# A gated block behind a selective scan: what follows the first norm is re-timed, and the last two units' work is rearranged

## The chip, the cores and the metric

The kernel runs on one core of one Trainium2 chip. The metric is the device time of one execution in microseconds. Five engines work side by side: TensorE (PE; PEld is its weight load), VectorE (DVE), ScalarE (ACT), GpSimd (POOL), and SyncE (SP), which issues nearly all DMA transfers. Each engine takes its instructions strictly in the order in which the program lists them. An instruction that waits holds up everything behind it on its engine.

## The reference

The input x is 4 sequences of 1024 rows of 256 numbers, all float32. In short:

```python
def _mamba(u, ...):                       # u = rmsnorm(layernorm(x))
    z, x, Bc, Cc, dt_raw = split(u @ in_proj_w.T)
    dt = softplus(dt_raw @ dt_proj_w.T + dt_proj_b)
    h = exp(dt_t * A) * h + (dt_t * x_t) * B_t      # step by step over the 1024 rows
    y_t = sum over 32 states of h * C_t
    return ((y + x * D_param) * silu(z)) @ out_proj_w.T

h = u0 + _mamba(rmsnorm(u0)); xn = rmsnorm(h)       # u0 = layernorm(x)
a = h + (silu(xn @ gate_w.T) * (xn @ up_w.T)) @ down_w.T
x = x + a
v = layernorm(x)
hidden = fwht(silu(v @ W1.T) * (v @ W3.T))          # 1024 wide
x = x + hidden @ W2.T
```

The Walsh-Hadamard transform is folded into W2 once, at the start.

## The kernel before

**Units.** The 4096 rows are cut into 8 units of T = 512 rows (`us`), two to a sequence. The second unit of a sequence (units 1, 3, 5, 7, "odd") carries the scan's state over from the first ("even").

**The scan.** 256 channels by 32 states by 512 rows are too much for one tile, so each unit's scan is 16 quarters (`q`, 128 in all). A quarter holds four tiles of 128 lanes by 512 rows (`da`, 128x2048). A quarter takes two *ticks*. In each tick DVE multiplies u by B for two of the four tiles (`bx`, line 765) and runs two scans (line 774). So a unit is 32 ticks and the whole scan is ticks 0 to 255. The text counts ticks within the unit that is being scanned, t0 to t31. Around a quarter:

- SP loads `da` (dt spread over lanes, 1 MB) into one of four buffers, three quarters ahead (`dma_da`), and `ub` in halves.
- ACT turns `da` into exp(dt*A), two tiles a tick, one quarter ahead (line 741).
- POOL multiplies the scanned quarter by C in one instruction (`times_c`, line 784), in the even tick that follows the scan. In even units it first copies the last column to `carry` (line 783).
- PE sums over the states in the odd tick after that (`sum_states`, line 795, "the sum" below). The sum frees the `da` buffer, so the next load of `da` waits for it.
- Every eighth quarter a new B has to be in PSUM (`pb`, one buffer). `copy_b` (line 754) copies it in t15 and t31: before, DVE did it in t15 and ACT in t31.

**Everything else.** It is written into the same ticks with `at(tick, lane, function)`. In a tick the lanes are issued in a fixed order: PE, ACT, the tick's `bx`, ACTb, two exps, a scan, DVE, a scan, POOL0, `times_c`, POOL, the sum, PEend, ACTend, SP, the scan's loads, SPend. So the order on every engine is set by hand. The work is of two kinds:

- `pre(u, H)`: what a unit needs before its scan, which starts at tick H. LayerNorm and first rmsnorm of x in one (`row_stats`, `small`, `un`), transposes (`ut`), the projections `pe_x`, `pe_dt`, `pe_c`, and the transfers through DRAM that spread rows over lanes (`dma_xb`, `dma_xr`, `dma_dt`, `dma_u`, `dma_c`). All of it runs during the scan one and two units earlier.
- `post(u, E, other)`: what follows a unit's scan, which ended at tick E. `wo` (with `add_rows`), `row_stats` and `small2` (rmsnorm), `hn`, transposes (`ht`), two `gated` calls for gate and up (product `m`), `wd` by `add_rows`, the second LayerNorm (`small3`, `hn`, `xt`), three `gated` calls for W1 and W3 (product `g`), W2 by `add_rows` in four blocks of 128 rows, and `store`. This runs during the scan of the next unit, and for the last unit after all scans (the *tail*). `gated` also computes z of the unit `other`.

A `gated` call puts its projections (two matmul instructions each) two to a tick on PE, the silus on ACT a tick later, the copies `up` (line 270) two ticks later and the products on POOL (line 274) two and three ticks later. Silu, Exp and Softplus need an activation table load when ACT goes from one to another.

`add_rows` can bring its result into `hr` in two ways: DVE adds out of PSUM (line 316), or ACT copies it out (`evict`, line 321) and POOL adds (line 325).

**What the buffers tie.** PSUM: four `dense` banks in rotation, two for `bx`, one for `pb`, one for the sums. `big` (m, then g) has one buffer, `tok` (un, hn) has one, `T` (ut, ht, yt, xt) has three.

In before, offsets in `post` are written from E and those in `pre` from H: gated m at E+10 and E+13, wd at E+18, gated g at E+26, E+29, E+32, W2 at E+36, store at E+43; `un` at H-32, its transposes at H-30, `pe_x` at H-24, `dma_xr` at H-19 and H-17, `pe_dt` and the first `pe_c` at H-16. With E = H = a multiple of 32 these are t10, t13, t18, t26, t29, then t0, t4 to t7, t11; and t0, t2, t8, t13, t15, t16.

Of the kernel before, what the change touches and what calls it, by code (L numbers as in the profile page):

```python
# [27 lines left out]
def tile_block(ctx: ExitStack, tc: tile.TileContext, a, out):  # L28
# [130 lines left out]
        nc.scalar.mul(w2h[:, k : k + 2, :], pw, 1.0 / 32.0)  # L159


    def row_stats(u, src, ts, centred=True):

        if 0 in ts:
            u["mv"] = sm.tile([P, 2, TT], F32, tag="mv", name="mv")
        for t in ts:
            junk = p1.tile([P, DM], F32, tag="junk", name="junk")
            nm, ms = u["mv"][:, 0, t : t + 1], u["mv"][:, 1, t : t + 1]
            if centred:
                nc.scalar.activation(  # L170
                    junk, src[:, t, :], AF.Identity, scale=-1.0 / (16 * DM), accum_out=nm
                )
            nc.scalar.activation(  # L173
                junk,
                src[:, t, :],
                AF.Square,
                bias=nm if centred else 0.0,
                scale=1.0 / 16,
                accum_out=ms,
            )  # L180
# [64 lines left out]
    def gated(tick, u, dst, wa, wb, chunks, src, z=None):  # L245


        g = [{} for _ in chunks]
        pe_z, act_z = z[0]["z"] if z else (None, None)

        def pe(i, name, w):
            c, n = chunks[i]
            if n < P:

                both = project(W[w], c * P, 2 * n, u[src])
                g[i]["pg"], g[i]["pu"] = both, both[n:]
            else:
                g[i][name] = project(W[w], c * P, n, u[src])

        def silus():  # L260
            for i, (_, n) in enumerate(chunks):
                g[i]["si"] = p3.tile([P, T], F32, tag="si", name="si")
                nc.scalar.activation(g[i]["si"][:n], g[i]["pg"][:n], AF.Silu)  # L263
            if z:
                act_z(z[1])

        def up(i):
            n = chunks[i][1]
            g[i]["up"] = p3.tile([P, T], F32, tag="up", name="up")
            nc.scalar.copy(g[i]["up"][:n], g[i]["pu"][:n])  # L270

        def product(i):
            c, n = chunks[i]
            nc.gpsimd.tensor_tensor(u[dst][:n, c, :], g[i]["si"][:n], g[i]["up"][:n], ALU.mult)  # L274

        three = len(chunks) == 3
        steps = [(i, *s) for s in (("pg", wa), ("pu", wb)) for i in range(len(chunks))]
        steps = [s for s in steps if chunks[s[0]][1] == P or s[1] == "pg"]
        late = z and len(steps) == 6
        steps = [(pe, *s) for s in steps]  # L280
        if z:
            steps.insert(3, (pe_z, z[1]))
        for k, step in enumerate(steps):
            at(tick + k // 2, "PE", *step)
        at(tick + 1, "ACTend" if three else "ACT", silus)
        at(tick + 2, "ACT", up, 0)
        for i in range(1, len(chunks)):
            if i == 2 and late:
                at(tick + 3, "ACT", up, i)
            else:  # L290
                at(tick + 2, "ACTend", up, i)
        at(tick + 2, "POOL", product, 0)
        for i in range(1, len(chunks)):
            at(tick + 3, "POOL", product, i)

    def add_rows(tick, u, lhs, rhs, per_tick, lane="PE", on_pool=False):

        po = {}

# [25 lines left out]
            nc.gpsimd.tensor_tensor(hr, hr, po[i][0], ALU.add)  # L325

        for t in range(TT):
            at(tick + t // per_tick, lane, pe, t)
            if t % 2:
                after = tick + t // per_tick + 1  # L330
                if on_pool:
                    at(after, "ACTend", evict, t // 2)
                    at(after + 1, "POOL", add_pool, t // 2)
                else:
                    at(after, "DVE", add, t // 2)


    def pre(u, H):
# [218 lines left out]
            return  # L557
        if H == 32:

            at(0, "ACTend", lambda: row_stats(u, u["x"], (0, 1)))  # L560
            at(1, "ACTend", lambda: row_stats(u, u["x"], (2, 3)))
            at(3, "POOL", small)
            at(5, "POOL", small_end)
            at(4, "ACT", un, (0, 1))
# [2 lines left out]
            at(6, "ACTend", transposed, u, "ut")  # L567
        else:
            at(H - 54, "SP", load_x, u)
            at(H - 45, "ACTend", lambda: row_stats(u, u["x"], (0, 1)))  # L570
            at(H - 43, "ACTend", lambda: row_stats(u, u["x"], (2, 3)))
            at(H - 39, "POOL", small)
            at(H - 37, "POOL", small_end)
            at(H - 32, "ACT", un, (0, 1))
            at(H - 31, "ACT", un, (2, 3))
            at(H - 30, "PE", lambda: transposes(u, s["un"]))
            at(H - 30, "ACTend", transposed, u, "ut")
        at(H - 24, "PE", pe_x)
        at(H - 23, "ACT", act_x)
        at(H - 22, "SP", dma_xb)  # L580
        at(H - 19, "SPend", dma_xr, 0)
        at(H - 17, "SPend", dma_xr, 1)
        at(H - 16, "PE", pe_dt)
        at(H - 16, "PE", pe_c, 0)
        if H == 32:
            for h in range(2):
                at(H - 11, "PE", pe_z, h)
# [16 lines left out]
    def post(u, E, other):  # L604


        s = {}

        def hr(ts):
            if 0 in ts:  # L610
# [20 lines left out]
            scaled_rows(s["tok"], u["hr"], s[scale], s[bias] if bias else None, range(TT))  # L631

        def big(name):
            u[name] = p1.tile([P, 8, T], F32, tag="big", name=name)

        def store():
            b, c = u["b"], u["c"]
            nc.sync.dma_start(
                out=out[b, c * T : (c + 1) * T, :].rearrange("(t p) d -> p t d", p=P), in_=u["hr"]
            )  # L640

        at(E + 3, "ACT", hr, (0, 1))
        at(E + 4, "ACT", hr, (2, 3))
        add_rows(
            E + 3,
            u,
            lambda: [u["yt"][:, k, :] for k in range(2)],
            lambda: [W["wo"][:, k, :] for k in range(2)],
            4,
            "PEend",  # L650
            on_pool=u is not us[-1],
        )
        at(E + 5, "ACTend", lambda: row_stats(u, u["hr"], (0, 1), False))
        at(E + 6, "ACTend", lambda: row_stats(u, u["hr"], (2, 3), False))
        at(E + 7, "POOL", small2)
        at(E + 8, "ACT", hn, "r3", None)
        at(E + 9, "PE", lambda: transposes(u, s["tok"]))
        at(E + 9, "ACTend", transposed, u, "ht")
        at(E + 9, "POOL", lambda: nc.gpsimd.tensor_tensor(u["hr"], u["hr"], u["x"], ALU.add))
        at(E + 10, "PE", big, "m")  # L660
        sizes = [min(P, DFF - c * P) for c in range(6)]
        chunks = list(enumerate(sizes))
        for i in range(2):
            gated(E + 10 + 3 * i, u, "m", "wg", "wu", chunks[3 * i : 3 * i + 3], "ht",
                  (other, i) if other else None)
        add_rows(
            E + 18,
            u,
            lambda: [u["m"][:n, c, :] for c, n in enumerate(sizes)],
            lambda: [W["wd"][:n, c, :] for c, n in enumerate(sizes)],  # L670
            1,
        )
        at(E + 20, "ACTend", lambda: row_stats(u, u["hr"], (0, 1)))
        at(E + 22, "ACTend", lambda: row_stats(u, u["hr"], (2, 3)))
        at(E + 23, "POOL", small3)
        at(E + 24, "ACT", hn, "r4", "nm")
        at(E + 25, "PE", lambda: transposes(u, s["tok"]))
        at(E + 25, "ACTend", transposed, u, "xt")
        at(E + 26, "PE", big, "g")
        chunks8 = [(c, P) for c in range(8)]  # L680
        for i in range(3):
            gated(E + 26 + 3 * i, u, "g", "w1", "w3", chunks8[3 * i : 3 * i + 3], "xt")
        add_rows(
            E + 36,
            u,
            lambda: [u["g"][:, c, :] for c in range(8)],
            lambda: [w2h[:, c, :] for c in range(8)],
            1,
            on_pool=u is not us[-1],
        )  # L690
        at(E + 43, "SPend", store)


    an = nega.rearrange("p (h j b a) -> p h j b a", h=2, j=4, b=4)
# [53 lines left out]
    def carry_of(s):  # L748
        return s["u"]["carry"][:, s["h"], s["j"], :, s["g"]]

    def copy_b(q):
        u, h = qs[q]["u"], qs[q]["h"]
        u["pb"] = ps_b.tile([P, T], F32, tag="b", name="pb")
        (nc.vector.tensor_copy if h else nc.scalar.copy)(u["pb"], u["br", h])  # L754

    def times_b(q, b0):
        s = qs[q]
# [15 lines left out]
        start = 0.0 if u["c"] == 0 else carry_of(s)[:, b : b + 1]  # L773
        nc.vector.tensor_tensor_scan(da, da, s["bx"][:, b % 2, :], start, ALU.mult, ALU.add)  # L774

    def times_c(q):
        s = qs[q]
        u = s["u"]
        if u["c"] == 0:
# [1 line left out]
                kept = p2.tile([P, 2, 4, 4, 2], F32, tag="carry", name="carry")  # L781
                u["carry"] = us[us.index(u) + 1]["carry"] = kept
            nc.gpsimd.tensor_copy(carry_of(s), s["da"][:, :, T - 1])
        nc.gpsimd.tensor_tensor(  # L784
            s["da"], s["da"], s["cr"].unsqueeze(1).broadcast_to([P, 4, T]), ALU.mult
        )

    def sum_states(q):
        s = qs[q]
# [22 lines left out]
        )  # L812

    def y_z(u, h):
        nc.gpsimd.tensor_tensor(u["yt"][:, h, :], u["yt"][:, h, :], u["zs"][:, h, :], ALU.mult)


    for k, u in enumerate(us):
# [29 lines left out]
        at(10 + i, "PE", hadamard_end, 2 * i)  # L848
    for q in range(8, NQ, 8):
        at(2 * q - 8, "SPend", dma_br, q)  # L850

        at(2 * q - 1, "DVE" if q // 8 % 2 else "ACTb", copy_b, q)

    def has(q):
        return 0 <= q < NQ

    tick = min(todo)
    while todo:
# [12 lines left out]
        if has(q):  # L871
            scan(q, 2 * half + 1)
        run(tick, "POOL0")
        if half == 0 and has(q - 1):
            times_c(q - 1)
        run(tick, "POOL")
        if half == 1 and has(q - 1):
            sum_states(q - 1)
# [83 lines left out]
```

## Time and profile before

| | us |
|---|---|
| median of 3 timed executions | 1166.05 (1165.02 to 1168.84) |
| the profiled execution's own time | 1173.07 |
| its span | 1171.2 |
| first `bx` of units 1, 2, 3, 4 | 158.67, 285.07, 415.20, 543.38 |
| first `bx` of units 5, 6, 7 | 671.46, 800.02, 925.55 |
| end of the last scan | 1053.61 |
| from there to the end of the span (the tail) | 117.6 |

The page gives the busy time of each engine and its share in 40 slices. The timeline lists instructions with the idle time of the engine before each, in square brackets, and what ended that idle time. The list of waits adds these up. From the timeline one also reads how late an engine is against its plan: the start of an instruction less the start of DVE's `bx` of the tick in which it is planned. For the sums on PE this lateness is called PE's backlog below.

### The profile page before, as it was taken

The page shows a single profiled execution, that of the slowest core. Times are in us where ns is not written, and L with a number is a line of the kernel's source. Part 1 is how long each engine was busy: PE and PEld are TensorE (multiplying, and loading weights), DVE is VectorE, ACT ScalarE, POOL GpSimd, SP SyncE. Part 2 cuts the span into 40 slices and gives each one's busy share as a digit, 9 for nine tenths or more (in the row PEclk, how much of TensorE's full clock was granted, in tenths as well). Part 3 has the DMA queues.
Part 4 walks back from the last instruction along what each step waited for, and adds up shares of the span by engine and source line. Part 5 has one row for each costly group of instructions (what it writes and reads, how often), then busy time and mean ns, then how long its engine had stood idle before and what let it go on. Part 6 is the DMA issues. An engine that isn't in the chain of part 4 may idle for free.

```text
span 1171.2 us, 11883 instructions
## 1 busy us (share of the span) xinstructions
PE 959.6 (82%) x3374; PEld 456.5 (39%) x3374; DVE 962.9 (82%) x840; ACT 782.2 (67%) x1411; POOL 887.1 (76%) x515
## 2 busy tenths in 40 slices
PE   8464236969998799969996999979997987799978
PEld 3121012423634255423633364424543362336535
DVE  4897799999998989999999899999999899990000
ACT  3835556868768786779677786878685967563331
POOL 6675758878978888878977998789977898674312
PEclk9777558979899799979998899979997999789989
DMA  7989999898799889997799889988799789730000
GB/s 252 352 300 351 353 327 308 311 325 296 250 340 320 300 298 320 319 327 281 270 348 325 281 300 334 319 325 297 270 310 360 281 291 343 262 111 1 18 0 18
DMA packets 89441, 321.89 MB, mean 275 GB/s; under 512 B 9312, under 2 KB 20000, under 8 KB 73120
## 3 DMA queue, kind: packets, MB, share of 16 engines
q1 hardware_dynamic: 87520, 318.38, 77.1%
q10 hardware_dynamic: 1856, 2.75, 0.7%
q8 instruction: 27, 0.44, 0.1%
q14 instruction: 38, 0.31, 0.1%
HBM read 302.22 MB, written 18.87 MB: 274 GB/s over the span
## 4 chain that ended last, share of the span: by engine, by line
PE 25%; DMA 7%; DVE 6%; POOL 6%; issue 5%; ACT 4%; DVEq 0%; POOLq 0%; ACTq 0%; SPq 0%
PE dense L226 14%; PE dense L306 8%; DMA da<-dtd 5%; POOL da L784 4%; DVE da L774 3%; DVE bx L765 3%; PE py L795 3%; DMA ub<-ud 2%; ACT da L741 1%; POOL m L274 1%; POOL g L274 1%; DVE hr L316 0%; ACT up L270 0%; ACT L741 0%; ACT junk L173 0%
## 5 line engine op out<-in xcount | busy, mean ns | idle before, releaser
L784 POOL TENSOR_TENSOR da<-da,cr 128x2048 f32<-128x2048 f32 x128 | 580.0, 4531 | 86.8 <-DVE da L774 22.5
L741 ACT ACTIVATE da<-da,nega 128x512 f32<-128x512 f32 x508 | 334.4, 713 | 170.8 <-DMA da<-dtd 159.3
L774 DVE TENSOR_TENSOR_SCAN da<-da,carry,bx 128x512 f32<-128x512 f32 x256 | 315.7, 1268 | 20.0 <-DVE bx L765 7.6
L774 DVE TENSOR_TENSOR_SCAN da<-da,bx 128x512 f32<-128x512 f32 x256 | 300.2, 1209 | 37.0 <-ACT da L741 21.3
L765 DVE TENSOR_TENSOR bx<-ub,pb 128x1024 f32<-128x1024 f32 x254 | 312.2, 1229 | 20.3 <-ACT pb L754 9.3
L795 PE MATMUL py<-da,rsel 128*32 128x512 f32 x1024 | 162.5, 712 | 159.4 <-POOL da L784 159.4
L226 PE MATMUL dense<-xt,w 128*128 128x512 f32 x512 | 238.4, 621 | 1.4 <-ACT si L263 1.4
L226 PEld LDWEIGHTS dense<-xt,w 128*128 128x128 f32 x512 | 99.4, 199 | 145.9 <-issue 123.4
L795 PEld LDWEIGHTS py<-da,rsel 128*32 128x32 f32 x1024 | 21.4, 115 | 243.0 <-POOL da L784 201.2
L306 PE MATMUL dense<-w2h,g 128*128 128x256 f32 x512 | 113.4, 380 | 0.0
L274 POOL TENSOR_TENSOR g<-si,up 128x512 f32<-128x512 f32 x64 | 80.5, 1272 | 32.3 <-ACT up L270 32.2
L306 PEld LDWEIGHTS dense<-w2h,g 128*128 128x128 f32 x512 | 96.8, 190 | 18.4 <-ACT ev L321 2.5
L306 PE MATMUL dense<-wd,m 128*128 128x256 f32 (+1 forms) x384 | 98.2, 400 | 0.9 <-POOL m L274 0.9
L316 DVE TENSOR_TENSOR hr<-hr,dense 128x512 f32<-128x512 f32 x20 | 13.4, 669 | 99.9 <-PE dense L306 99.9
L226 PE MATMUL dense<-ut,win 128*128 128x512 f32 x192 | 94.7, 625 | 0.2 <-ACT ut L220 0.2
L270 ACT COPY up<-dense 128x512 f32<-128x512 f32 x112 | 63.4, 579 | 46.8 <-PE dense L226 46.4
L274 POOL TENSOR_TENSOR m<-si,up 128x512 f32<-128x512 f32 (+1 forms) x48 | 60.2, 1270 | 43.5 <-ACT up L270 43.5
L226 PE MATMUL dense<-ht,wg 128*128 128x512 f32 x192 | 87.7, 600 | 3.4 <-ACT ht L220 3.4
L306 PEld LDWEIGHTS dense<-wd,m 128*128 128x128 f32 (+1 forms) x384 | 68.6, 192 | 37.6 <-issue 20.6
L263 ACT ACTIVATE si<-dense 128x512 f32<-128x512 f32 x112 | 60.7, 596 | 28.4 <-PE dense L226 25.5
L226 PE MATMUL dense<-ht,wu 128*128 128x512 f32 x160 | 72.8, 600 | 4.8 <-ACT si L263 4.8
L741 ACT ACT_TABLE_LOAD x44 | 56.5, 1283 | 4.8 <-DMA da<-dtd 4.0
(95 smaller groups left out, 798.6 us busy)
## 6 DMA issues: line engine op xcount, KB each, us to landing
da<-dtd SPq DMA_DIRECT2D x127, 1024.0 KB
ub<-ud SPq DMA_DIRECT2D x254, 512.0 KB
cr<-cd SPq DMA_DIRECT2D x64, 256.0 KB
x<-in_x SPq DMA_DIRECT2D x8, 512.0 KB
dtd<-dt SPq DMA_DIRECT2D x16, 256.0 KB
ud<-du SPq DMA_DIRECT2D x16, 256.0 KB
cd<-cc SPq DMA_DIRECT2D x16, 256.0 KB
out<-hr SPq DMA_DIRECT2D x8, 512.0 KB
```

The lines of the kernel that those rows point to most:

```text
L226: nc.tensor.matmul(dst[:n], lhsT=w[:, k, col : col + n], rhs=src[:, k, :], start=(k == 0), stop=(k == 1),)
L263: nc.scalar.activation(g[i]["si"][:n], g[i]["pg"][:n], AF.Silu)
L270: nc.scalar.copy(g[i]["up"][:n], g[i]["pu"][:n])
L274: nc.gpsimd.tensor_tensor(u[dst][:n, c, :], g[i]["si"][:n], g[i]["up"][:n], ALU.mult)
L306: nc.tensor.matmul(po[t // 2][:, t % 2, :], lhsT=left[k][:, t * P : (t + 1) * P], rhs=right[k], start=(k == 0), stop=(k == n - 1),)
L316: nc.vector.tensor_tensor(hr, hr, po[i], ALU.add)
L741: nc.scalar.activation(da, da if q else s["u"]["pdt", b], AF.Exp, scale=an[:, s["h"], s["j"], b, s["g"] : s["g"] + 1],)
L765: nc.vector.tensor_tensor(s["bx"], s["ub", b0 // 2], u["pb"].unsqueeze(1).broadcast_to([P, 2, T]), ALU.mult)
L774: nc.vector.tensor_tensor_scan(da, da, s["bx"][:, b % 2, :], start, ALU.mult, ALU.add)
L784: nc.gpsimd.tensor_tensor(s["da"], s["da"], s["cr"].unsqueeze(1).broadcast_to([P, 4, T]), ALU.mult)
L795: nc.tensor.matmul(u["py"][32 * b : 32 * b + 32, :], lhsT=rsel[:, 2 * s["j"] + s["g"], :], rhs=s["da"][:, b, :], start=first, stop=last,)
```

## The change

1. **Re-timing, units 0 to 5** (`many`). Wo and the first statistics stay where they are, and so does `small2`. From `hn` on everything of `post` is a tick later (F = E+1): gated m at t11 and t14, wd at t19, gated g at t27, t30 and t1, W2 at t5 to t8, the store at t12. The second `hn` goes to ACTend. In `pre`, `un` and its transposes come two ticks later (t2, t3, t4), `pe_x`, `act_x`, `dma_xb`, both `dma_xr`, `pe_dt` and the first `pe_c` a tick later; `act_dt`, `act_c`, `make_u` and the other transfers stay.
2. **Units 6 and 7** run `post` from `hn` on two ticks sooner (F = E-2), their statistics at E+4 and `small2` at E+5. Unit 6's wo is added by DVE instead of ACT and POOL.
3. **W2 of unit 6**: of its four blocks, two go around unit 7's wo (E+34 and E+36 of unit 6), two behind unit 7's wd (E+52). The last unit's m and g get tiles of the `da` pool, so that unit 6's g can stay in `big`.
4. **copy_b** is on ACT everywhere but for q = 8 and q = 120.
5. **The end of the scan**: the last quarter's product with C is issued in two halves, the first a tick sooner; the last `y_z` is done by DVE; the last unit's store goes out in two halves.

```diff
-    def add_rows(tick, u, lhs, rhs, per_tick, lane="PE", on_pool=False):
+    def add_rows(ticks, u, lhs, rhs, lane="PE", on_pool=False):
...
         for t in range(TT):
-            at(tick + t // per_tick, lane, pe, t)
+            at(ticks[t], lane, pe, t)
             if t % 2:
-                after = tick + t // per_tick + 1
+                after = ticks[t] + 1
...
-            at(H - 32, "ACT", un, (0, 1))
-            at(H - 31, "ACT", un, (2, 3))
-            at(H - 30, "PE", lambda: transposes(u, s["un"]))
-            at(H - 30, "ACTend", transposed, u, "ut")
-        at(H - 24, "PE", pe_x)
-        at(H - 23, "ACT", act_x)
-        at(H - 22, "SP", dma_xb)
-        at(H - 19, "SPend", dma_xr, 0)
-        at(H - 17, "SPend", dma_xr, 1)
-        at(H - 16, "PE", pe_dt)
-        at(H - 16, "PE", pe_c, 0)
+            at(H - 30, "ACT", un, (0, 1))
+            at(H - 29, "ACT", un, (2, 3))
+            at(H - 28, "PE", lambda: transposes(u, s["un"]))
+            at(H - 28, "ACTend", transposed, u, "ut")
+        at(H - 23, "PE", pe_x)
+        at(H - 22, "ACT", act_x)
+        at(H - 21, "SP", dma_xb)
+        at(H - 18, "SPend", dma_xr, 0)
+        at(H - 16, "SPend", dma_xr, 1)
+        at(H - 15, "PE", pe_dt)
+        at(H - 15, "PE", pe_c, 0)
...
+        last = u is us[-1]
+
+        many = us.index(u) < len(us) - 2
...
         def big(name):
-            u[name] = p1.tile([P, 8, T], F32, tag="big", name=name)
+            if last:
+
+                tiles = [pda.tile([P, 4, T], F32, tag="da", name=name) for _ in range(2)]
+                u[name] = [tiles[c // 4][:, c % 4, :] for c in range(8)]
+            else:
+                tile = p1.tile([P, 8, T], F32, tag="big", name=name)
+                u[name] = [tile[:, c, :] for c in range(8)]
...
-            on_pool=u is not us[-1],
+            on_pool=many,
         )
-        at(E + 5, "ACTend", lambda: row_stats(u, u["hr"], (0, 1), False))
-        at(E + 6, "ACTend", lambda: row_stats(u, u["hr"], (2, 3), False))
-        at(E + 7, "POOL", small2)
-        at(E + 8, "ACT", hn, "r3", None)
+        for i in range(2):
+            at(E + (5 + i if many else 4), "ACTend", row_stats, u, "hr", (2 * i, 2 * i + 1), False)
+
+        F = E + 1 if many else E - 2
+        at(E + 7 if many else E + 5, "POOL", small2)
+        at(F + 8, "ACT", hn, "r3", None)
...
         add_rows(
-            E + 18,
+            range(F + 18, F + 22),
...
-        at(E + 24, "ACT", hn, "r4", "nm")
+        at(F + 24, "ACTend" if many else "ACT", hn, "r4", "nm")
...
+        o2 = (E + 34, E + 36, E + 52, E + 52) if not (many or last) else range(F + 36, F + 40)
         add_rows(
-            E + 36,
+            o2,
...
-        at(E + 43, "SPend", store)
+        if last:
+            at(o2[1] + 1, "SPend", store, 0, 2)
+            at(o2[3] + 1, "SPend", store, 2, 2)
+        else:
+            at(o2[3] + 4, "SPend", store)
...
+    def by_vector(q):
+
+        return q in (8, NQ - 8)
+
     def copy_b(q):
         u, h = qs[q]["u"], qs[q]["h"]
         u["pb"] = ps_b.tile([P, T], F32, tag="b", name="pb")
-        (nc.vector.tensor_copy if h else nc.scalar.copy)(u["pb"], u["br", h])
+        (nc.vector.tensor_copy if by_vector(q) else nc.scalar.copy)(u["pb"], u["br", h])
...
     def y_z(u, h):
-        nc.gpsimd.tensor_tensor(u["yt"][:, h, :], u["yt"][:, h, :], u["zs"][:, h, :], ALU.mult)
+        eng = nc.vector if u is us[-1] and h else nc.gpsimd
+        eng.tensor_tensor(u["yt"][:, h, :], u["yt"][:, h, :], u["zs"][:, h, :], ALU.mult)
...
-        if half == 0 and has(q - 1):
+        if half == 0 and has(q - 1) and q < NQ:
             times_c(q - 1)
+        elif q in (NQ - 1, NQ) and tick >= 2 * NQ - 1:
+
+            if tick <= 2 * NQ:
+                times_c(NQ - 1, (slice(0, 2) if half else slice(2, 4),))
```

## The prediction

> **What bounds the kernel.** First the page: which engine is busy, and when.
>
> ```profile
> PE 959.6 (82%) x3374; PEld 456.5 (39%) x3374; DVE 962.9 (82%) x840; ACT 782.2 (67%) x1411; POOL 887.1 (76%) x515
> DVE  4897799999998989999999899999999899990000
> ```
>
> DVE is full during the scan and idle in the last tenth. So there are two bounds: DVE until the last scan ends at S = 1053.61, then a chain through PE. A tick on DVE is one `bx` (1.23) and two scans (2.33, or 2.45 with carry): 3.7 or 3.83, and .7 more where DVE has an add, a y_dx or a copy. Second, the DVE timeline, where it falls short of that:
>
> ```profile
> 345.40 0.67 DVE L754 COPY pb<-br 128x512 f32<-128x512 f32 x1
> 355.30 2.33 DVE L774 TENSOR_TENSOR_SCAN da<-da,bx 128x512 f32<-128x512 f32 x2 [3.05 <-ACT da L741]
> 415.20 1.23 DVE L765 TENSOR_TENSOR bx<-ub,pb 128x1024 f32<-128x1024 f32 x1 [3.16 <-ACT pb L754]
> 671.46 1.23 DVE L765 TENSOR_TENSOR bx<-ub,pb 128x1024 f32<-128x1024 f32 x1 [4.09 <-ACT pb L754]
> 925.55 1.23 DVE L765 TENSOR_TENSOR bx<-ub,pb 128x1024 f32<-128x1024 f32 x1 [2.04 <-ACT pb L754]
> 936.98 0.75 DVE L810 SCALAR_TENSOR_TENSOR yt<-xr,dpar,py 128x512 f32<-128x512 f32 x1 [0.96 <-PE py L795]
> ```
>
> The largest stalls wait for copy_b on ACT, at the end of the even units 2, 4, 6. Third, ACT there:
>
> ```profile
> 668.64 0.60 ACT L263 ACTIVATE si<-dense 128x512 f32<-128x512 f32 x1 [0.96 <-PE dense L226]
> 670.35 0.58 ACT L270 COPY up<-dense 128x512 f32<-128x512 f32 x1 [1.11 <-PE dense L226]
> 670.84 0.60 ACT L754 COPY pb<-br 128x512 f32<-128x512 f32 x1
> ```
>
> copy_b stands behind a silu and an `up` that wait for PE, and PE is late. Fourth, why (waits, SP's own included):
>
> ```profile
> PE py L795 <- POOL da L784: 159.4, 56, 10.8
> ACT da L741 <- DMA da<-dtd: 159.3, 51, 10.3
> SPq L704 <- PE py L795: 286.2, 95, 7.3
> ```
>
> It is a ring: a late sum frees `da` late, the load and ACT's exps come late, then POOL's products, then the sum. Fifth, the tail:
>
> ```profile
> 1061.31 1.06 PE L795 MATMUL py<-da,rsel 128*32 128x512 f32 x8
> 1067.79 13.98 PE L306 MATMUL dense<-w2h,g 128*128 128x256 f32 x64
> 1082.93 5.42 PE L226 MATMUL dense<-ht,wg 128*128 128x512 f32 x12 [0.29 <-ACT ht L220]
> 1120.88 2.80 PE L213 MATMUL dense<-ident,hn 128*128 128x128 f32 x8 [5.86 <-ACT hn L200]
> ```
>
> The last sum waits for PE's W1/W3 work although POOL was done at 1058.35; then unit 6's whole W2 stands before unit 7's norm; later PE idles 5.86 for the second norm.
>
> **The scan, part by part.** I measure PE's backlog at the sums and carry it on: backlog + PE's work between two sums - DVE's two ticks (7.5 in an even unit, 8.2 with an extra). PE's rows: a projection 1.78, a W2 block 3.5, a wd block 3.0, wo 3.6, transposes 1.1, pe_dt 1.9, a sum 1.0. Read in unit 4, t3 to t17: .4, 6.3, 6.9, 4.8, 6.0, 8.2, 9.1, 6.2. The rule gives 6.9 for t7, 5.1 for t9 and 8.4 for t13, so it holds.
>
> In the new order t5 has wo, transposes and one W2 block before its sum (9.2) where it had wo and two blocks. From .9 at t3 (POOL's end) it gives t5 2.6; t7 3.2; t9 (a block and pe_x) 3.8; t11 2.0; t13 2.6; t15 (five projections) 5.0; t17 (two projections, pe_dt, pe_c) 5.8; t19 1.6. If wo waits for y_z as in unit 4 (5.16 instead of 3.6), each is 1.6 higher. The peak falls from 9.1 to 5.0-6.6 and comes at t15-t17.
>
> - *copy_b at t31.* Before it now stand the `up`s of t29 instead of a silu and an `up` of t30/31: at least two projections less of PE. It is in time while the backlog at t29 is below about 9. Stalls removed: 3.16 + 4.09 + 2.04.
> - *copy_b at t15* leaves DVE: 6 x .67 = 4.0. On ACT it follows an `up` that needs PE's first projection of t14: sum 1.0, projection 1.8, `up` .6, exps 1.33, copy .6. DVE waits only if the backlog at t13 is over 5.7; I have 2.6-4.2. If that cover goes, each us over costs a us in six units. Behind it on ACT stand the tick's exps. It also waits for the tick's `bx` (1.23 into the tick); ACT was 2.5 to 11.6 into t15 when it came to its exps there, so this holds nothing up.
> - *y_dx at t2* (about 1 in units 3, 5, 7): it waits if the backlog at t1 exceeds 5.2. The work before that sum is the same, but `hn` now follows two exps and `xt` comes a tick later, so the first two projections of t27 stand just before t27's sum. From the 3.5-4.1 that odd units show at t27 to t31 I get 5-6.4 at t1: 0 to 1.2 per unit, .7 taken.
> - *Softplus at t17*: pe_dt is now in the tick of act_dt. PE ends it at backlog(t15) - 1.0 after t17's start; then a softplus and a table load (1.28), so exps start at backlog + 1.4. They must start by 8.8. With 5.0-6.6: no stall, little margin.
> - *Statistics to small3*: `small2` keeps its tick and `hn` moves, so the 3.30 that ACT stood before it in unit 4 (at 575.28) becomes slack. POOL's products move to odd ticks: product 0 fills the 2.9 between two `times_c` and the next two follow the second one. small3 moves behind t24's `times_c` with small right behind: `times_c` of t26 up to 1 late.
> - *SP*: xbd, the eight xr and the store each go behind one more ub load (.6 of issue). Their reader, du on POOL, has its tick kept at t19 and ran at t20+1.5 in unit 4; xr now goes out at t14 and t16, the later one for the unit's second half. Nothing, up to 1 in a unit if xr lands late.
> - *DMA*: 307 GB/s over the 130 us from 710 at a busy share of .87 is 39.9 MB a unit; in 122.5 us that is 326 GB/s. From 30 to 60 it moved 354. It fits, but between 60 and 190, at 328 GB/s, DVE stalled 3 to 4 us at a time. I add 1 to each even unit.
>
> Unit by unit, from its first `bx` to the next: without stalls an even unit is 125.53 (unit 6) - 2.04 - .3 - .67 = 122.5, an odd one 126.40 (unit 1) - .67 = 125.7. So units 1 to 6 lose .7, 7.6, 2.5, 5.6, 2.9, 3.0 = 22.3. Unit 7 loses .96 at y_dx and gains two adds of .69 that unit 6's wo puts on DVE: +.4. Unit 0, held by weight loads, I leave at nothing (between -2 and +2). Residues: 1.7 in three even units, .7 in four odd ones, 7.9. Scan: -22.3 + .4 + 7.9 = -14.0; ends -22 and 0.
>
> **The tail, from S.** Before, the last sum started at S+7.7 and wo ended at S+14.3. Now W1/W3 of unit 6 ends two ticks sooner, inside the scan. POOL: `times_c` of quarter 126, two products (2.5), the two halves (2.27 each, half of 4.53): S+4.0, not far from the old S+4.7, since those products stand before. Sum 1.9, y_dx .8, y_z on DVE .7: yt at S+7.6. Meanwhile PE does a W2 block to S+9.5, then wo to S+13.0: 1.3 sooner. From wo's end to gated it was 15.0, because 14.0 of W2 stood there. Now add .8, statistics 1.1, small2 1.5, the evict behind the second block (3.5 + .8 after wo, so it decides), `hn` to gated 3.3 (as 1120.22 to 1123.50): 7.6. Gain 8.7 in all. At the second norm 8.5 passed from wd's end to gated; now W2's last two blocks (7.07) and their evict (.8) stand before `hn`: 7.9 + 3.3 = 11.2, loss 2.7. The half store at the end: gain .5. Tail: -6.5; ends -4 (both norms wait longer) and -9 (no loss at the second).
>
> Here the trace has y_z as POOL's 1.26 at 1063.35, and no DVE instruction with two inputs in SBUF. The Trainium skill (SBUF — State Buffer, "SBUF: two separate sides") speaks against moving it: such a DVE instruction and a POOL one that reads SBUF exclude each other for a whole instruction. Unit 6's last two products run then, so y_z would wait up to 1.27, yt at S+8.9; PE's W2 block ends at S+9.5, so the sum stays.
>
> **Sum.** -14.0 - 6.5 = -20.5 on the profiled 1173.07, which is .6% above the median; I carry the difference to the median: 1166 - 20 = 1146.
>
> **Rivals.**
> - *The ring closes elsewhere.* POOL's small3 or late `da` loads keep even units late and only copy_b (4.0) and the tail (6.5) pay, less residues of 1-2: about 1157. For: 159 us of ACT waiting for `da`. Against: odd units run the same loads and show none of the large stalls. 0.20.
> - *Slower: softplus at t17 holds the exps.* If the backlog at t15 is over 7.4, DVE waits for the rest in six units. It cancels the 20.5 at 10.8. Unit 2 had 11.3 before, which gives 3.9 x 6 = 23: 1169. Against: the two W2 blocks that made that backlog are spread. 0.10.
> - *Everything goes*: no residues, tail -9: 1166 - 31 = 1135 to 1139. 0.13.
> - The forecast, 1140 to 1153: 0.55; other mishaps 0.02.
>
> Range: 1136 leaves about .06 below, 1162 about .13 above. A measurement tells about 0.3% (3.5 us) from no change. Faster by more: .55 + .13 + .18 = .86; within: .02 + .04 = .06; slower .08.
>
> **What would show it.** Right: no wait of over 1 us for copy_b at the ends of units 2, 4, 6; even units near 124; sums' backlog under 7 at t15 and t17; the last sum near S+4, 64 matmuls of W2 in three pieces, unit 7's first gated near S+20.6, the span's end near S+111. Wrong: DVE idle at t17 to t19 or t22 behind exps, waits for copy_b in t15, an idle PE of over 3 before the tail's wo.

## The result and the profile after

The changed kernel takes 1177.48 us (1174.43 to 1178.96), before's executions beside it 1166.05: a ratio of 1.0094 with an interval of 1.0065 to 1.0122. It is 11.4 us slower, where 20 faster was forecast.

| | before | after |
|---|---|---|
| the profiled execution's own time | 1173.07 | 1177.48 |
| end of the last scan, S | 1053.61 | 1065.35 |
| the tail, from S to the span's end | 117.6 | 110.35 |
| units 1 to 7, first `bx` to the next (unit 7: to S) | 126.4 130.1 128.2 128.1 128.6 125.5 128.1 | 127.4 130.0 131.0 128.2 134.8 131.0 128.3 |

The tail came out as forecast (-7.3, forecast -6.5). The scan did not: +11.7 between these two executions, forecast -14.0. Of the +11.7, units 1 to 7 lost 15.7 and unit 0 gained 4.0. Before's profiled execution is moreover a late one: the median of its kernel was 1164.43, 1164.29 and 1163.90 beside the later experiments.

The page of the changed kernel, busy time and DVE's row over the span:

```profile
PE 962.6 (82%) x3374; PEld 457.0 (39%) x3374; DVE 962.1 (82%) x837; ACT 789.3 (67%) x1417; POOL 883.8 (75%) x513
DVE  4887899998998989899988989799978999993000
```

DVE did the same 962 us of work. So the loss is idle time. Its waits in the whole span, changed kernel (what waited, for what, us in total, times, longest):

```profile
DVE yt L833 <- PE py L818: 30.1, 13, 5.3
DVE da L794 <- ACT da L757: 20.8, 26, 3.7
DVE bx L785 <- ACT pb L774: 6.4, 4, 3.3
```

The same lines of before:

```profile
DVE yt L810 <- PE py L795: 12.5, 7, 8.9
DVE da L774 <- ACT da L741: 21.5, 18, 4.2
DVE bx L765 <- ACT pb L754: 9.3, 3, 4.1
```

The line that grew is y_dx (line 833), which waits for the sum on PE. Its longest entry, 5.3 after and 8.9 before, lies in the tail, so the scan's share went from 3.6 to 24.8. I sorted the idle times over .3 us of units 1 to 7 by tick (copy_b under the tick in which it is planned; the `bx` that waits for it is the next tick's first instruction):

| place | before | after |
|---|---|---|
| t31, `bx` for copy_b | 9.3 | none |
| t15, `bx` for copy_b | none | 6.1 |
| t18, scan for exps (before: t17) | 4.4 | 5.5 |
| t18, y_dx for the sum of t17 | none | 16.0 |
| t2, y_dx for the sum of t1 | 2.9 | 8.8 |

y_dx runs twice a unit, once for each half of the channels: at t18 for the first half and at t2 of the next unit for the second. At t18 it waits 1.4 in unit 1 and 2.8 to 3.0 in each of units 2 to 6. Unit 4, DVE's timeline in the changed kernel:

```profile
612.93 1.23 DVE L785 TENSOR_TENSOR bx<-ub,pb 128x1024 f32<-128x1024 f32 x1
615.58 1.22 DVE L794 TENSOR_TENSOR_SCAN da<-da,bx 128x512 f32<-128x512 f32 x1 [1.43 <-ACT da L757]
619.76 0.75 DVE L833 SCALAR_TENSOR_TENSOR yt<-xr,dpar,py 128x512 f32<-128x512 f32 x1 [2.95 <-PE py L818]
```

And PE beside it, changed kernel:

```profile
609.80 1.06 PE L818 MATMUL py<-da,rsel 128*32 128x512 f32 x8
610.80 3.70 PE L227 MATMUL dense<-ht,wu 128*128 128x512 f32 x8
614.34 1.88 PE L407 MATMUL dense<-raw,dtw 128*128 128x512 f32 x4
616.63 1.98 PE L227 MATMUL dense<-ut,win 128*128 128x512 f32 x4 [0.41 <-ACT up L271]
618.54 1.07 PE L818 MATMUL py<-da,rsel 128*32 128x512 f32 x8
```

The sum at 609.80 is that of t15, that at 618.54 the one of t17. POOL's product for the latter was done at 612.3. So it waits for what stands before it on PE: two projections, pe_dt (line 407) and pe_c, which itself stood .41 for an `up` on ACT. DVE's t17 began at 609.23, so the backlog is 9.3. ACT, changed kernel, same moment:

```profile
616.01 1.17 ACT L271 COPY up<-dense 128x512 f32<-128x512 f32 x2
617.20 1.28 ACT L416 ACT_TABLE_LOAD   x1
618.50 1.27 ACT L416 ACTIVATE dt<-dense,dtb 128x512 f32<-128x512 f32 x2
619.78 1.28 ACT L757 ACT_TABLE_LOAD   x1
621.07 1.33 ACT L757 ACTIVATE da<-da,nega 128x512 f32<-128x512 f32 x2
```

Softplus (line 416) needs the same pe_dt; ACT comes to it behind two `up`s, and the exps behind it end at 622.4. DVE shows no wait for them, but only because y_dx has already held it until 619.76. Whether that second wait is as long as the first is what the fourth and fifth experiment ask.

### The profile page after: what moved, and what is told of

Read it like the earlier page. It is cut to its first block, busy times and chain, and to the rows that moved or that the text cites. A ratio compares the mean times of both kernels' runs of the same rounds, so it can differ in the third digit from the quotient of the medians.

```text
span 1175.7 us, 11888 instructions
## 1 busy us (share of the span) xinstructions
PE 962.6 (82%) x3374; PEld 457.0 (39%) x3374; DVE 962.1 (82%) x837; ACT 789.3 (67%) x1417; POOL 883.8 (75%) x513
## 5 line engine op out<-in xcount | busy, mean ns | idle before, releaser
L794 DVE TENSOR_TENSOR_SCAN da<-da,bx 128x512 f32<-128x512 f32 x256 | 299.9, 1208 | 33.5 <-ACT da L757 18.1
L818 PE MATMUL py<-da,rsel 128*32 128x512 f32 x1024 | 157.1, 685 | 164.5 <-POOL da L807 164.4
L227 PE MATMUL dense<-xt,w 128*128 128x512 f32 x512 | 243.6, 630 | 5.8 <-ACT xt L221 5.6
L307 PE MATMUL dense<-w2h,g 128*128 128x256 f32 x512 | 116.4, 383 | 6.8 <-ACT ut L221 6.2
L307 PEld LDWEIGHTS dense<-w2h,g 128*128 128x128 f32 x512 | 95.7, 190 | 32.1 <-issue 11.7
L227 PE MATMUL dense<-ht,wg 128*128 128x512 f32 x192 | 90.7, 617 | 5.7 <-ACT ht L221 5.7
L227 PE MATMUL dense<-ht,wu 128*128 128x512 f32 x160 | 77.8, 628 | 8.1 <-ACT si L264 8.0
L227 PEld LDWEIGHTS dense<-ut,win 128*128 128x128 f32 x192 | 36.9, 200 | 58.7 <-issue 41.9
```

Of the source, the lines that this page charges most:

```text
L227: nc.tensor.matmul(dst[:n], lhsT=w[:, k, col : col + n], rhs=src[:, k, :], start=(k == 0), stop=(k == 1),)
L307: nc.tensor.matmul(po[t // 2][:, t % 2, :], lhsT=left[k][:, t * P : (t + 1) * P], rhs=right[k], start=(k == 0), stop=(k == n - 1),)
L818: nc.tensor.matmul(u["py"][32 * b : 32 * b + 32, :], lhsT=rsel[:, 2 * s["j"] + s["g"], :], rhs=s["da"][:, b, :], start=first, stop=last,)
```

## The experiments

The first theory was that PE's order at t15 to t18 costs the time: the sum behind pe_dt and pe_c holds y_dx. Rivals: SP, which in the changed kernel stands 24.6 us waiting to load x; copy_b on ACT; and exps that would be as late without y_dx. Each ratio below is to before's executions on the same chip and in the same comparison (median 1164.43 for the first four experiments, 1164.29 for softplus alone, `pre` alone, copy_b back on DVE and the even ends, 1163.90 for the other three). All diffs are against the changed kernel unless they say otherwise.

### The tail alone

Parts 1 and 4 are undone: units 1 to 6 are scanned under before's own plan. Parts 2, 3 and 5 stay. The same edit takes back all the other lines of part 1 in `pre`.

```diff
-        F = E + 1 if many else E - 2
+        F = E if many else E - 2
-        at(F + 24, "ACTend" if many else "ACT", hn, "r4", "nm")
+        at(F + 24, "ACT", hn, "r4", "nm")
-        at(H - 15, "PE", pe_dt)
-        at(H - 15, "PE", pe_c, 0)
+        at(H - 16, "PE", pe_dt)
+        at(H - 16, "PE", pe_c, 0)
...
-        return q in (8, NQ - 8)
+        return q // 8 % 2 == 1
```

> The changed kernel with parts 1 and 4 undone: units 0 to 5, pre and copy_b as before, the last two units, unit 6's W2 and the end of the scan as changed. If the loss is in the re-timing of units 0 to 5, the scan ends within 3 us of before's 1053.6 and the tail stays near the changed kernel's 110.4 (before: 117.6): about 1166 - 7 = 1159. If the tail's parts cost something inside the scan (unit 7 has two more adds on DVE and starts its work earlier), unit 7 takes 131 or more instead of 128 and the time comes to 1162 to 1166.

Measured: 1153.74, ratio .9919 (.9887 to .9951), tail 108.9, S 1042.87. That is below both expectations, and it beats both kernels. So parts 1 and 4 together cost 11.4 + 10.7 = 22 us, and parts 2, 3 and 5 earn at least what the tail was said to earn. This kernel has four executions, one of them 7 above the rest: by the ratios the 22 are 20, and what is set against this kernel below is 2 to 4 less by the ratios than by the medians. Waits of DVE, tail alone:

```profile
DVE yt L833 <- PE py L818: 9.0, 7, 5.3
DVE bx L785 <- ACT pb L774: 4.7, 3, 1.9
```

The last line is worth a second look. Under the same plan for units 1 to 6, copy_b at t31 cost 4.7 here and 9.3 in before's profiled execution, and the exps at t17 nothing over .3 here and 4.4 there. About 9 us of what the prediction wanted to remove did not come with the plan, but with that one execution. It is not the only such scatter: the profiled execution took 6.1 less than its kernel's median with pe_dt and softplus later, 4.9 less with `post` alone, 5.1 more with copy_b back on DVE. Differences of some 5 us between two profiles are therefore not read as an edit's doing below; a wait that comes back in every unit is.

### x loaded later

POOL's sum of `hr` and x moved with part 1 to t10, and frees the buffer into which SP loads the next x. SP's own waits, changed kernel:

```profile
SPq L720 <- PE py L818: 348.4, 108, 8.8
SPq L77 <- POOL hr L671: 16.4, 3, 7.1
SPq L77 <- POOL carry L803: 8.2, 2, 4.1
```

The prediction had not listed this. It could be the ring's cause, since every `da` load stands behind it.

```diff
-            at(H - 54, "SP", load_x, u)
+            at(H - 51, "SP", load_x, u)
```

> The changed kernel with the load of x three ticks later (t13 instead of t10). In the changed kernel SP stood 24.6 us in five waits before this load, since its buffer is freed by POOL's hr + x, which has moved to t10; the loads of da and ub stand behind it. Theory 'SP held by x': these waits go, the sums' backlog at t13 and t15 falls from 6 to 12 to about 4 and 6.6, the waits for copy_b at t15 (5 to 6 us in units 2, 5, 6) go and y_dx at t18 waits about 2 instead of 4: about 15 us less, 1162. Theory 'sum behind pe_dt' alone: t18 keeps its 4 us in units 2 to 6, and only the 5 to 6 us at t15 return: 1172.

Measured: 1176.73, ratio 1.011 (1.008 to 1.014). SP's waits for x, later load:

```profile
SPq L720 <- PE py L818: 347.6, 113, 6.8
SPq L77 <- DMA win<-in_win: 2.0, 1, 2.0
```

The 24.6 us are gone, and y_dx at t18 still waits 16.1 in all. 24.6 us of SP standing still had cost nothing that can be measured. This theory falls.

### pe_dt, pe_c and softplus later

```diff
-        at(H - 15, "PE", pe_dt)
-        at(H - 15, "PE", pe_c, 0)
+        at(H - 14, "PE", pe_dt)
+        at(H - 14, "PE", pe_c, 0)
-        at(H - 15, "ACT", act_dt, 0)
-        at(H - 15, "ACT", act_dt, 1)
-        at(H - 14, "ACT", act_c, 0)
+        at(H - 13, "ACT", act_dt, 0)
+        at(H - 13, "ACT", act_dt, 1)
+        at(H - 12, "ACT", act_c, 0)
```

`make_u` and the transfers behind it go two ticks later as well.

> The changed kernel with pe_dt and the first pe_c a tick later (t18, behind the sum of t17), and softplus, the copy of C, du and their three transfers two ticks later. Theory 'sum behind pe_dt': the sum of t17 no longer stands behind them, its backlog falls from 9.3 to about 5.6, y_dx at t18 waits under 1 instead of 4: 18 us less, 1159. Theory 'exps behind softplus': as softplus moves too, the exps of t17 are early as well, and this run cannot part the two; e4 does. Theory 'SP held by x' alone: the backlog at t15 stays at 8 to 11 and with it the waits at t15 (5 to 6 us) and some 2 to 3 us at t18: 1168.

Measured: 1163.45, ratio .9978 (.9958 to .9998): 14 us of the loss return. PE in unit 4:

```profile
601.06 1.06 PE L818 MATMUL py<-da,rsel 128*32 128x512 f32 x8
602.06 3.70 PE L227 MATMUL dense<-ht,wu 128*128 128x512 f32 x8
605.69 1.06 PE L818 MATMUL py<-da,rsel 128*32 128x512 f32 x8
606.69 1.98 PE L407 MATMUL dense<-raw,dtw 128*128 128x512 f32 x4
```

The sum of t17 now stands before line 407. DVE at t18, same kernel:

```profile
606.84 1.22 DVE L794 TENSOR_TENSOR_SCAN da<-da,bx 128x512 f32<-128x512 f32 x1 [1.43 <-PE py L818]
607.98 0.72 DVE L833 SCALAR_TENSOR_TENSOR yt<-xr,dpar,py 128x512 f32<-128x512 f32 x1
```

No wait at y_dx, one of 1.43 ahead of it. The trace puts this one down to the sum, but a scan reads no sum; ACT's exps began at 606.03, and the scan starts when the first of them is done. In units 1 to 7 together such waits for exps come to 4.4 at t18; .8 are left for copy_b at t15, and 10.3 at t2.

### y_dx of the first half a tick later

This takes away only what y_dx waits for, and leaves PE and ACT as they are.

```diff
-            at(2 * q + 4, "DVE", y_dx, u, s["h"])
+            at(2 * q + 4 + (s["h"] == 0), "DVE", y_dx, u, s["h"])
```

> The changed kernel with only the y_dx of t18 a tick later (t19). If DVE's wait there is y_dx's alone, the 21 us of t18 in units 1 to 7 return: 1157. If the exps of t17 are as late by themselves (they start 8.1 us into t18 in unit 4 and must be there at t19), DVE waits for them at t19 instead, 2 to 3 us in each of units 2 to 6, and only 7 to 10 us return: 1168.

Measured: 1173.69, ratio 1.0068 (1.0045 to 1.0091). At most 4 return, less than either expectation, and the interval overlaps that of the changed kernel. DVE, unit 4:

```profile
622.91 1.22 DVE L794 TENSOR_TENSOR_SCAN da<-da,bx 128x512 f32<-128x512 f32 x1 [2.65 <-ACT da L757]
624.05 0.72 DVE L833 SCALAR_TENSOR_TENSOR yt<-xr,dpar,py 128x512 f32<-128x512 f32 x1
```

And ACT:

```profile
619.58 1.27 ACT L416 ACTIVATE dt<-dense,dtb 128x512 f32<-128x512 f32 x2
622.16 1.33 ACT L757 ACTIVATE da<-da,nega 128x512 f32<-128x512 f32 x2
```

y_dx no longer waits, and the scan of t19 waits 2.65 for exps: 2.5 to 2.7 in each of units 1 to 6, 15.6 in all. The second wait is as long as the first, and was hidden behind it.

### Softplus later, pe_dt not

The other half of the third experiment: `act_dt`, `act_c` and what follows them two ticks later, pe_dt and pe_c left at H-15.

```diff
-        at(H - 15, "ACT", act_dt, 0)
-        at(H - 15, "ACT", act_dt, 1)
-        at(H - 14, "ACT", act_c, 0)
+        at(H - 13, "ACT", act_dt, 0)
+        at(H - 13, "ACT", act_dt, 1)
+        at(H - 12, "ACT", act_c, 0)
```

> The changed kernel with softplus, the copy of C, du and their transfers two ticks later, but pe_dt and pe_c left in t17, in front of the sum. If DVE's wait at t18 is PE's order (two projections, pe_dt and pe_c between the sums of t15 and t17), y_dx still waits 3 us for the sum in units 2 to 6 and only the 5.5 us that exps held at t18 return: about 1171. If softplus on ACT is the cause of both, the wait goes as it did when pe_dt moved too: 1160 to 1164.

Measured: 1171.85, ratio 1.0058 (1.0038 to 1.0079). ACT's exps are early now, done before 620. DVE, unit 4, all the same:

```profile
618.43 0.75 DVE L833 SCALAR_TENSOR_TENSOR yt<-xr,dpar,py 128x512 f32<-128x512 f32 x1 [2.95 <-PE py L818]
```

16.0 in all at this place, as in the changed kernel. The scan's wait for exps at t18 stays as well (5.1 for 5.5): these exps are those of t16 and stand behind an `up` that waits 2.37 for PE, not behind softplus. So what returned is not the 5.5 expected; in the profile copy_b at t15 fell from 6.1 to 1.8 and t2 from 8.8 to 6.4. With the two runs before it: taking away y_dx's wait alone returned 4, taking away softplus alone 6, and moving pe_dt and softplus, which takes away both waits, 14. At t18 two waits of like length lie on top of each other.

### The three edits of parts 1 and 4, one at a time

Each starts from the tail alone, and re-does one of them. First `pre` alone (from `un` to pe_c as in the changed kernel):

```diff
-        F = E + 1 if many else E - 2
+        F = E if many else E - 2
-        at(F + 24, "ACTend" if many else "ACT", hn, "r4", "nm")
+        at(F + 24, "ACT", hn, "r4", "nm")
-        return q in (8, NQ - 8)
+        return q // 8 % 2 == 1
```

> The changed kernel with unit 0 to 5's post and copy_b as before; pre stays re-timed (un at t2, pe_x at t9, pe_dt and pe_c in t17). Here only pe_dt and pe_c stand between the sums of t15 and t17, since gated's last two projections are back in t15. If it takes both moves together to hold y_dx, the backlog at t17 is 4 to 6, y_dx waits under 1 and the time is that of the tail alone, 1154 to 1157. If pe_dt in the tick of softplus is enough by itself, exps are late at t17 and DVE waits 1 to 3 us at t18 or t19 in units 1 to 6: 1162 to 1168.

Measured: 1161.66, ratio .9968 (.9953 to .9984), between the two expectations. Exps at t17 to t18 hold DVE 3.7 in all, y_dx not (.25 at most). In unit 4:

```profile
606.76 2.33 DVE L794 TENSOR_TENSOR_SCAN da<-da,bx 128x512 f32<-128x512 f32 x2 [1.76 <-ACT da L757]
```

That is some 8 us worse than the tail alone (6 by the ratios), of which these 3.7 are placed. The rest stays open.

Second, `post` alone, a tick later (pe_dt and pe_c at H-16 as before, but issued behind gated's last two projections, which now fall into the same tick):

```diff
-        at(H - 15, "PE", pe_dt)
-        at(H - 15, "PE", pe_c, 0)
+        at(H - 16, "PEend", pe_dt)
+        at(H - 16, "PEend", pe_c, 0)
...
-        return q in (8, NQ - 8)
+        return q // 8 % 2 == 1
```

> The first experiment's kernel with post of units 0 to 5 a tick later from hn on, as changed; pre and copy_b as before. pe_dt and pe_c keep t16, but behind gated's last two projections, which are now in t16 too, so PE's order from the sum of t15 to that of t17 is the changed kernel's: two projections, pe_dt, pe_c, sum. If that order is what holds y_dx, it waits 2 to 3 us at t18 in units 2 to 6 (12 to 16 us in all), y_dx waits at t2 as in the changed kernel (5 to 9 us), and the time is 1166 to 1172. If pre's shift is needed as well, 1156 to 1162.

Measured: 1176.58, ratio 1.0085 (1.0057 to 1.0113), some 4 above the upper expectation. This edit alone brings the whole loss, 12.7 + 10.7 = 23 against the tail alone. Unit 4:

```profile
620.64 0.75 DVE L833 SCALAR_TENSOR_TENSOR yt<-xr,dpar,py 128x512 f32<-128x512 f32 x1 [2.95 <-PE py L818]
```

The same 2.95 at the same place, 15.8 in all, and 7.7 at t2. For comparison, y_dx of that unit in the tail alone:

```profile
607.59 0.75 DVE L833 SCALAR_TENSOR_TENSOR yt<-xr,dpar,py 128x512 f32<-128x512 f32 x1 [0.25 <-PE py L818]
```

Third, copy_b alone, on ACT everywhere but at the two ends. `pre` and `post` are taken back as in the tail alone, and `by_vector` is left as the change has it:

```diff
-        F = E + 1 if many else E - 2
+        F = E if many else E - 2
-        at(H - 15, "PE", pe_dt)
+        at(H - 16, "PE", pe_dt)
...
         return q in (8, NQ - 8)
```

> The first experiment's kernel with copy_b of t15 on ACT in units 1 to 6, nothing else. In this plan the copy stands behind an up of t15 that needs PE's last but one projection of that tick, and the backlog at t13 is 5 to 8.5. DVE saves 4.0. By the prediction's limit of about 5.7, less the 3.6 us of two more projections in front, every unit waits: 2 to 5 us each in units 2, 4, 6 and 1 to 3 in the odd ones, 10 to 20 in all: 1160 to 1170. If ACT is far enough ahead, 1150.

Measured: 1161.11, ratio .9963 (.9941 to .9985), some 7 worse than the tail alone by the medians (5 by the ratios, whose intervals overlap), as expected. DVE waits 18.1 for it at t15. Unit 4, ACT's timeline:

```profile
601.54 0.58 ACT L271 COPY up<-dense 128x512 f32<-128x512 f32 x1 [0.72 <-PE dense L227]
602.03 0.60 ACT L774 COPY pb<-br 128x512 f32<-128x512 f32 x1
```

DVE's, same kernel:

```profile
602.65 1.23 DVE L785 TENSOR_TENSOR bx<-ub,pb 128x1024 f32<-128x1024 f32 x1 [3.97 <-ACT pb L774]
```

Behind an `up` that waits for PE, the copy is late, as it was at t31. The losses of the three edits, 8, 23 and 7, do not add up: together they cost 22.

And the changed kernel with copy_b back on DVE in t15:

```diff
-        return q in (8, NQ - 8)
+        return q // 8 % 2 == 1
```

> The changed kernel with copy_b of t15 back on DVE in units 1 to 6. This costs DVE 6 x 0.67 = 4.0 and takes away the waits for copy_b at t15 (2 to 6 us over units 2 to 6): between +2 and -2 us, 1175.5 to 1179. If the copy on ACT was what kept exps behind at t16 to t18, the waits at t18 fall as well and it comes to 1170 or less.

Measured: 1171.92, ratio 1.0061 (1.0042 to 1.0080). t15 shows no wait; t18 (20.3, was 21.5) and t2 (9.5, was 8.8) are much as they were. copy_b on ACT seems to cost in the changed kernel, too: 11.4 against 7.6 over before; the two intervals overlap, so this is not shown.

### Two attempts to go further

The tail alone, with copy_b on DVE also at the ends of the even units:

```diff
-        return q in (8, NQ - 8)
+        return q // 8 % 2 == 1 or q in (48, 80, 112)
```

> The kernel of the first experiment (only the last two units, W2 of unit 6 and the end of the scan changed) with copy_b at the ends of units 2, 4 and 6 on DVE as well. DVE pays 3 x 0.67 = 2.0 and no longer waits there for ACT (4.7 us in the first experiment's profile, 9.3 in before's): 2.7 to 7 us less than 1153.7, so 1147 to 1151. If the wait only moves to the exps behind it, 1153 to 1156.

Measured: 1155.80, ratio .9912 (.9888 to .9937). The waits at t31 are gone; the time can't be told from that of the tail alone (.9919).

The third experiment, with y_dx of the second half a tick later, to take away the 10.3 at t2 as well:

```diff
-            at(2 * q + 4, "DVE", y_dx, u, s["h"])
+            at(2 * q + 4 + (s["h"] == 1 and u is not us[-1]), "DVE", y_dx, u, s["h"])
```

> The third experiment's kernel (pe_dt and softplus behind the sum of t17) with the y_dx of t2 a tick later, but for the last unit. In the third experiment's profile y_dx waited 10.3 us at t2 over units 2 to 7. If that wait is y_dx's alone, 6 to 9 us return: 1155 to 1157. If wo, which needs y_z and so comes later on PE, makes the backlog at t5 grow by as much as DVE gains (3.8 a unit), exps or copy_b are late at t12 to t15 and nothing returns: 1161 to 1166.

Measured: 1160.93, ratio .9957 (.9935 to .9978). t2 shows nothing any more, but t15 14.0 and t18 6.6. Unit 4:

```profile
598.64 2.33 DVE L794 TENSOR_TENSOR_SCAN da<-da,bx 128x512 f32<-128x512 f32 x2 [2.69 <-ACT da L757]
603.00 1.23 DVE L785 TENSOR_TENSOR bx<-ub,pb 128x1024 f32<-128x1024 f32 x1 [2.03 <-ACT pb L774]
```

Backlogs of units 2 to 6 are 5.4 to 7.5 at t5 here (4.2 to 4.5 in the changed kernel) and 10 to 12.6 at t15. DVE no longer gives PE the pause at t2 in which it caught up, and waits later instead. Of 10.3 taken away at most 2.5 stay, and the two intervals overlap. The tail alone remains the fastest.

## Why the prediction was wrong, step by step

**The tail: right, but for one term.** The last sum, as PE ran it in the changed kernel, and what follows:

```profile
1069.50 1.05 PE L818 MATMUL py<-da,rsel 128*32 128x512 f32 x4 [1.25 <-POOL da L807]
1070.49 3.72 PE L307 MATMUL dense<-w2h,g 128*128 128x256 f32 x16
1074.05 3.62 PE L307 MATMUL dense<-wo,yt 128*128 128x256 f32 x16
1077.50 3.62 PE L307 MATMUL dense<-w2h,g 128*128 128x256 f32 x16
...
1084.45 6.79 PE L227 MATMUL dense<-ht,wg 128*128 128x512 f32 x12
1117.82 7.17 PE L307 MATMUL dense<-w2h,g 128*128 128x256 f32 x32
```

From S = 1065.35: the sum's second half at S+4.2 (said: S+4.0), wo's end S+12.3 (13.0), first gated S+19.1 (20.6), end S+110.35 (111). W2 stands in three pieces, and the 7.17 of its last one lies before the second norm, as priced. Up to the first gated 10.2 were gained (8.7 said), at the second norm 2.3 lost (2.7). Between them 1.4 were lost that no term had: the first gated's twelve matmuls took 6.79 instead of before's 5.42. PE had stood 1.14 for `hn`, and the granted clock from 1084 to 1086 was .50 (before: 1.00).

**copy_b at t31: right.** The waits of 3.16, 4.09 and 2.04 are gone. But they were mis-sized as a gain: the tail alone, under before's plan, shows 4.7 in place of 9.3. Of the 22.3 of removable stalls some 9 were one late execution's; "I carry the difference to the median" kept their full size while taking the median as base.

**"y_dx at t2 ... waits if the backlog at t1 exceeds 5.2": the step that failed.** The limit is right and was used at one place of two; at the other, t18, y_dx's wait was put at nothing, and no reason was given. The tick of t18 has the same form: the sum of t17 must be done when DVE comes to y_dx. In unit 4 it gives 9.3 - 5.2 = 4.1; DVE stood 1.43 + 2.95 = 4.4. The prediction's own table had 5.8 at t17, 7.4 if wo waits for y_z: .6 to 2.2 a unit, 4 to 13 in six units, without any new measurement. It was never entered. Measured: 16.0 for y_dx, and 5.5 ahead of it. Over the units of the changed kernel the limit gives DVE's wait at t18 (scan and y_dx together) to .3 and that at t2 to .2. Even the 6.2 that the prediction read in before at t17 of unit 4 was over 5.2; it did not show because DVE had first stood .91 for exps in t17. At t2 itself .7 a unit was taken, 4.9 in all, and 8.8 measured: the backlog was already 4.3 to 6.7 at t27, where 3.5 to 4.1 was carried on. The two projections there took 4.7 to 6.6 instead of 3.7, after PE had stood .4 to 2.4 for `xt`.

The sum closes. The forecast left 7.9 of waits in units 1 to 7; measured are 38.0 (idle times over .3). That is 30.1 more, and unit 0, left at nothing, was 4.0 shorter: 26, where the scan came out 25.7 over its forecast.

**The backlog's table: the rule held, the entries were low.** In unit 4, beside the higher branch, in which wo waits for y_z:

| | t5 | t7 | t9 | t11 | t13 | t15 | t17 | t19 |
|---|---|---|---|---|---|---|---|---|
| said, with that wait | 4.2 | 4.8 | 5.4 | 3.6 | 4.2 | 6.6 | 7.4 | 3.2 |
| measured | 4.5 | 5.1 | 5.7 | 4.2 | 6.0 | 8.3 | 9.3 | 2.3 |

That it is right to .3 up to t9 is luck. wo did not wait for y_z: it took 3.72, straight behind the sum of t3. But that sum began at 1.5 instead of .9, since two W1/W3 projections stood before it, and PE then stood 1.24 for ACT's copy of `ut` before the W2 block, which no branch had. From sum to sum the steps from there to t17 hold to .3, but for t13, which is 1.2 more. There PE had stood .96 for a silu, which stood on ACT behind exps that waited for a `da` load:

```profile
593.10 1.33 ACT L757 ACTIVATE da<-da,nega 128x512 f32<-128x512 f32 x2 [4.33 <-DMA da<-dtd]
596.40 3.70 PE L227 MATMUL dense<-ht,wu 128*128 128x512 f32 x8 [0.96 <-ACT si L264]
```

The buffer of that load is freed by the sum of t9, which ended at 585.7; SP issued the load at 585.9. So the ring that the prediction described in before closes here, at t12: in each of units 1 to 6 ACT stood 4.3 to 5.6 at that place. In units 5 and 6 PE's pause was 1.90 and 2.19, and the two projections behind it took longer, too:

```profile
727.86 5.40 PE L227 MATMUL dense<-ht,wu 128*128 128x512 f32 x8 [1.90 <-ACT si L264]
```

The granted clock from 730 to 732 was .50. Whether the pause brought this on is not shown: with x loaded later PE stood 1.99 at this place in unit 5, and the two took 3.70. Units 5 and 6 reach 9.9 and 11.6 at t15. The claim that the peak "falls from 9.1 to 5.0-6.6" is wrong: it did not fall.

**Softplus at t17, "no stall, little margin": wrong, and its rival right in mechanism.** "Exps start at backlog + 1.4" gives 8.3 + 1.4 = 9.7 for unit 4. They started at 621.07, 11.8 after t17's start. Two `up`s (1.17) stand on ACT before softplus, and there are two table loads of 1.28 around it, where the prediction counted one. The rival's price was 1169; y_dx one tick later, in which the exps are what DVE waits for, measured 1173.69. What no rival had is that y_dx would wait for the same length at the same place.

**copy_b at t15, a gain of 4.0: wrong.** It was argued from a backlog at t13 of 2.6 to 4.2 against a limit of 5.7. The limit held to .4; the backlog was too low. Measured 6.8 in unit 2, 6.0 in unit 4, 7.8 in unit 5 and 9.4 in unit 6; waits of 6.1 for 4.0 saved. Under before's plan the same step costs some 7.

**SP: right. DMA: not put to the test.** SP's delay, even the large one that was not listed, cost nothing that shows. The 326 GB/s of a unit in 122.5 were never asked for: from 671 to 806, the slowest unit, the share was .84 at 301 GB/s; before, from 672 to 800, .89 at 314. Even units were shortest with copy_b on DVE at the even ends, 123.8 to 124.2 in units 2, 4 and 6, and there the loads kept up (unit 4, from 534 to 658: 311 GB/s).

**Open.** In unit 5 the granted clock was .92 in those 135 us (.95 in before's 128); beyond the 1.7 of the two projections above, no run separates how much of that unit's 6 us is due to it. y_dx one tick later and softplus later were not run together, nor pe_dt behind the sum with softplus left in t17. Of the 8 us that `pre` alone costs, 3.7 are placed. The tail alone gains 10.7 where its tail is 8.7 shorter than before's profiled one; the other 2 are within the scatter. Whether a re-timing without both waits of t18 and without the one of t2 could pay was not shown: each wait that was taken away came back elsewhere in part.

## What to carry to other kernels

When a limit has been derived ("this instruction waits if the backlog exceeds 5.2"), it is to be applied at every tick where the same instruction stands. Agreement of a sum at a few points is no proof of its terms: here two delays that nobody had listed made up for a wait that did not come. Two waits of equal length at one place hide each other: removing either shows little, and an experiment with both is needed before a cause is acquitted. Stalls that one profiled execution shows are a gain only in so far as the same plan shows them again; here some 9 us of 22 did not come back.

## What was not expected of the hardware

A wait of 24.6 us on SP, whose queue carries nearly all loads, had no effect on the time that can be measured (x loaded later: 1176.73 against 1177.48).

`y_z` on DVE took 1.05, where the additions out of PSUM that the prediction priced it by take .69. DVE in the tail of the changed kernel:

```profile
1071.41 1.05 DVE L839 TENSOR_TENSOR yt<-yt,zs 128x512 f32<-128x512 f32 x1
```

POOL at that time:

```profile
1069.39 2.52 POOL L275 TENSOR_TENSOR g<-si,up 128x512 f32<-128x512 f32 x2
```

POOL's products end at 1071.91, so the two overlap by .5. The Trainium skill (SBUF — State Buffer, "SBUF: two separate sides") would let the one wait for the other's whole instruction. Read as a full wait, that would be .5 and then .69, 1.19 in all, or an idle time before it; neither shows. In all twelve kernels with y_z on DVE the overlap is .5 and y_z takes 1.04 or 1.05, so no run tells a lock from an instruction that is simply longer with both inputs in SBUF: it is not settled. The sum was not touched, since PE's W2 block ran until 1074.05.
